# A transformer layer on one core: the first loads, the first tile, phase 3's pools and down's last terms rearranged

## The chip, the cores and the metric

The kernel runs on one core of one Trainium2 chip. The metric is the device time of one launch in microseconds (us). The core has a matrix engine (PE, with its weight loads shown as PEld), a vector engine (DVE), a scalar engine (ACT), a general engine (POOL) and a queue engine (SP) that issues most of the transfers. Each engine takes its instructions in the order in which they were written down for it.

## The reference

All data is float32. `x` is 2 x 1024 tokens of 512 features. After a layernorm, two branches read the same normed tokens and are added to `x`:

```python
xn = _layernorm(x, axis=-1)
# attention without a softmax over tokens
Q = elu(xn @ wq.T + bq) + 1; K = elu(xn @ wk.T + bk) + 1; V = xn @ wv.T + bv
KV = einsum('bhsd,bhse->bhde', K, V); K_sum = sum(K, axis=-2)
attn = (Q @ KV / (Q . K_sum + 1e-08)) @ wo.T + bo
# gated feed-forward, 1376 wide, with low-rank additions
scores = sigmoid(xn @ W_router); w = the two best of 8 experts, normed
gate = xn @ W_gate + lora_shared + sum_e w_e * lora_e     # rank 8 each
up   = xn @ W_up   + lora_shared + sum_e w_e * lora_e
hidden = silu(gate) * up
ffn = hidden @ W_down + lora_shared + sum_e w_e * lora_e
return x + attn + ffn
```

## The kernel before

Tokens go in 16 tiles of 128; `TILES` orders them so that tiles 2m and 2m+1 form a pair. The big products are not made directly: each is split in 2 x 2 blocks and made of seven block products with sums before and after (Strassen's scheme in Winograd's form), so much of DVE's, ACT's and POOL's work is block sums.

Names used below. `load_x(n)` (L146) sends tile n into a ring of four buffers. `norm(n)` (L285) writes the normed tile `xn` on DVE, after `moments`, `variances` (whose square root is on ACT, L264) and `reciprocals`. `transpose_x(n)` (L296) turns it on PE into a PSUM bank, which ACT copies into `xnT` (L302). A PSUM bank is named by a tag (`pt`, `ua`, `x`, `lo`).

**Phase 1, keys.** The loads at L150 to L159 are issued from SP in the order x0, x1, wk0, wk1, x2, wk2, wk3, x3; ACT issues the router's weights and the bias `bk`, the latter read 128 times into all partitions. Eighteen transposes of a unit matrix run on PE first (L245). Tiles 0 and 1 are projected directly (`project_k`, L344: products `pk`, bias added by DVE at L363), and POOL sums blocks of `wk` (`key_weight_sums`, L314). Pairs 1 to 7 use `k_pair` (L406) with the seven products (L424). `elu_min` and `elu_k` (L329 to L337) turn a key tile into elu(k)+1 on DVE, ACT and DVE; `accumulate` (L391) then adds its outer product with `xn` into four banks `pg`. `hooks` (L675) hang other work at named places ("n", "a", "b") of a pair: loads of the next weights, the block sums of `wq` (`query_weight_sums`), the block sums of pair 0's tokens (`pair_token_sums(0)`).

**Phase 2** forms KV, the queries, the denominators, the routing weights, and the last 96 columns of gate and up (`rest`, L1023). Its `gated_rows` stores `hr` tiles to DRAM (L1039), the last one after the second batch.

**Phase 3** (from L1454): for j in 0..4 and both batches, `unit(j, b)` (L1213) makes 2 x 128 columns of gate and up by seven outer products, five of which are split once more (`Inner`, L1168 to L1204), and stores the hidden tiles. Three pools are opened for it, in the order `up_`, `hp`, `p3`; each lies above the one before in the memory that phases 1 and 2 leave. `p3` holds `wi2` (written by POOL at L1142) and `ti56_1` (L1098); `hp` holds the hidden tiles `h`. POOL's order at the start is: `wi` sums of p=3, `wi2` sums, `ti23_0`, `token_sums_1`, `ti56_1`, `ti23_1`.

**Phase 4, down** (from L1577): four units u of 2 x 256 tokens. `emit_unit` makes seven products into seven PSUM banks (order 1, 6, 5, 2, 7, 3, 4) over five pairs of blocks of W_down (`wd`), then two of the attention's output (`kvo`); `ph` collects the hidden tiles times the experts' down factors and DVE weights it to `had` (L1616). Banks 1, 6 and 5 then go to sums (ACT L1633, POOL L1634 and L1636, DVE L1635 to L1639), while PE adds two kinds of low-rank terms to banks 2, 7, 3 and 4: `hr` (97 rows) and `had` (64 rows, rows 0 to 63 for one group of tokens and 64 to 127 for the other). DVE adds these banks to x (L1655) and SP sends the result (L1659). The next unit writes the same banks again. At the end of unit 1 the second batch's `kvo` is loaded and POOL makes its block differences (`block_diffs`, L1358) before its share of the sums.

The order on PE, DVE, ACT and POOL is that of the program text; SP's is the order in which its transfers were placed.

Of the kernel before, what the change touches and what calls it, by code (L numbers as in the profile page):

```python
# [37 lines left out]
def layer_kernel(  # L38
# [112 lines left out]
    load_x(0)  # L151
    load_x(1)
    nc.scalar.dma_start(out=wk_sb[:, :, D:], in_=by_chunk(w_router))
    bk_sb = p1.tile([P, D], F32, name="bk_sb")
    nc.scalar.dma_start(out=bk_sb, in_=bk.partition_broadcast(P))
    for c in range(NC):
        nc.sync.dma_start(out=wk_sb[:, c, 0:D], in_=wkT[ts(c, P), :])
        if c % 2:
            load_x(2 + c // 2)  # L159

# [4 lines left out]
    def load_factors():  # L165
        hold(a_in[:, 0, 0, 0:1])
        for i, a in enumerate((a_gate, a_up)):
            nc.sync.dma_start(out=a_in[:, :, i, :], in_=by_chunk(a))
        hold(ad_sb[:, 0, 0:1])
        nc.sync.dma_start(out=ad_sb[:, 0:FULL, :], in_=by_chunk(a_down[0 : FULL * P, :]))  # L170
        nc.sync.dma_start(out=ad_sb[0:REST, FULL, :], in_=a_down[RC, :])
# [110 lines left out]

    xns = {}

    def norm(n):  # L285

        k = n % 6
        xns[n] = (
            p1w.tile([P, D], F32, tag=f"xn{k}", name=f"xn{n}", bufs=1)
            if k < 4 else p2w.tile([P, D], F32, tag=f"qt{k - 2}1", name=f"xn{n}", bufs=1)  # L290
        )
        nc.vector.tensor_scalar(
            xns[n], x_sb[n], mv[:, n, 0:1], rstd[:, n : n + 1], ALU.subtract, ALU.mult
        )

    def transpose_x(n, tag="pt"):  # L296
        i = TILES[n]
        pt = bank(f"pt{i}", [P, NC, P], tag)
        for c in range(NC):
            nc.tensor.transpose(pt[:, c, :], xns[n][:, ts(c, P)], ident)  # L300
        for k in range(2):
            nc.scalar.copy(xnT[i // TPBATCH][k][:, :, ts(i % TPBATCH, P)], pt[:, 2 * k : 2 * k + 2, :])  # L302

# [35 lines left out]
    def k_tile(n):  # L339
        return p1w.tile([P, D], F32, tag="kt", name=f"kt{n}", bufs=4)  # L340

    LO, HI = slice(0, HD), slice(HD, D)

# [62 lines left out]
    def k_pair(m, late, hooks={}):  # L406
# [68 lines left out]
        nc.vector.tensor_add(ka[:, LO], ka[:, LO], lo)  # L475
        sums = pair_token_steps(2) if m == 1 else iter(())
        next(sums, None)
        ea = elu_min(ka, f"ek{na}") if m > 1 else None
        nc.vector.tensor_add(kb[:, HI], ua[:, 0:HD], bk_sb[:, HI])
        nc.vector.tensor_copy(lb, ua[:, HD:])  # L480
        ea = ea or elu_min(ka, f"ek{na}")
        list(sums)
        elu_k(ka, ea)
        eb = elu_min(kb, f"ek{nb}")
# [176 lines left out]
    for n in range(2):  # L661
# [3 lines left out]
        load_x(n + 4)  # L665
    transpose_x(0)
    wq_sums, sums1 = query_weight_sums(), token_sums(1)
# [4 lines left out]
    def routed(n):  # L672
# [3 lines left out]
        (1, "b"): [lambda: load_weights(wq_sb, wqT)],  # L676
        (2, "n"): [lambda: next(wq_sums), load_factors],
        (2, "b"): [lambda: next(wq_sums), lambda: load_weights(wv_sb, wvT)],
        (3, "n"): [lambda: next(wq_sums), lambda: next(wq_sums)],
        (3, "b"): [lambda: load_weights(wo_sb, woT), lambda: pair_token_sums(0), gather_factors, make_spread],  # L680
        (4, "b"): [lambda: fin.append(Finish(0, pg, ksum)), lambda: fin[0].copies()],
# [12 lines left out]
    for m in range(NTILE // 2):  # L694
        if m == 0:
            moments(2, 1)
            variances(2, 1)
            reciprocals()
            norm(2)
            load_x(6)  # L700
            moments(3, 1)
            ka = project_k(0, [[(0, "lo"), (1, "ua")]], lambda: transpose_x(1))
            variances(3, 1)
            key_weight_sums()
            ea = elu_min(ka, "ek0")
            reciprocals()
# [26 lines left out]

    bgu_sb = ffn.tile([2 * ER, DFF], F32, name="bgu_sb")
    for i, w in enumerate((b_gate, b_up)):
        nc.sync.dma_start(out=bgu_sb[i * ER : (i + 1) * ER, :], in_=w[0:ER, :])
# [717 lines left out]
    ph3 = ExitStack()  # L1454
    up_ = pool(ph3, "u", bufs=10)
    hp = pool(ph3, "hp", bufs=3)
    p3 = pool(ph3, "p3")
    ti56_1 = p3.tile([P, 2, 4, TH], F32, name="ti56_1")
# [118 lines left out]
    def emit_unit(u, loaded, last):  # L1577
# [44 lines left out]
        if u == 1:  # L1622
            kvo_next = load_kvo(1)
            for t in kvo_next:
                block_diffs(t)
            kvo[:] = kvo_next

# [16 lines left out]
        for pp in ((2, 7), (3, 4)):  # L1644
            for p in pp:
                g, w, _ = left[p]
                for q in range(NQ):
                    term(p, q, hr[:, g, ts(q, P)], w)
            for q in range(NQ):
                for p in pp:  # L1650
                    g, _, w = left[p]
                    rows = slice(g * ER, (g + 1) * ER)
                    term(p, q, had[rows, ts(q, P)], w[rows, :], stop=True)
        for t, d, p in ((x1, d1, 2), (x2, d2, 7), (x2, d1, 7), (x1, d2, 3), (x2, d1, 4)):
            nc.vector.tensor_add(t[:, :, d], t[:, :, d], ps[p])  # L1655
            if p == 7 and d is d1:
                continue
            first = first1 if t is x1 else first2
            nc.sync.dma_start(  # L1659
                out=out[first : first + UT, d].rearrange("(q p) d -> p q d", p=P), in_=t[:, :, d]  # L1660
            )
        if not last:
# [66 lines left out]
```

## Time and profile before

| | |
|---|---|
| median of 3 runs | 743.76 us (743.66 to 744.42) |
| the profiled execution: its own time, its span | 744.27 us, 742.5 us |
| PE busy | 730.5 us, 98% of the span |
| DVE, ACT, POOL busy | 484.6, 195.9, 161.0 us |
| from PE's last product to the span's end | 4.7 us |

The span runs from the first to the last instruction that the profiler saw; 1.77 us of the launch lie outside it. A line of a timeline gives the start, the duration, the engine, the line of the code, the operation, what it writes and reads with the sizes, how many were merged, and in brackets the idle time before it with what ended it. A line of the waits gives who waited for whom, the total, how often, and the longest. A float32 product leaves two records on PE.

### The profile page before, as it was taken

How to read it: one execution, taken by the hardware profiler on the slowest of the kernel's cores; microseconds unless marked ns; L12 is line 12 of the kernel's file. 1: busy time of each engine (PE TensorE's matmuls, PEld its weight loads, DVE VectorE, ACT ScalarE, POOL GpSimd, SP SyncE). 2: the span in 40 equal slices, each digit the busy share in tenths (PEclk: the TensorE clock that was granted, in tenths of full speed). 3: DMA queues.
4: the chain of work that ended last, by engine and by line, in shares of the span. 5: the costliest groups of instructions: out<-in, count | busy, mean ns of one | idle time of the engine just before them, and what ended most of it. 6: DMA issues, size and time to landing. Idle time of an engine off the chain costs nothing.

```text
span 742.5 us, 8737 instructions
## 1 busy us (share of the span) xinstructions
PE 730.5 (98%) x3078; PEld 489.6 (66%) x3078; DVE 484.6 (65%) x1044; ACT 195.9 (26%) x421; POOL 161.0 (22%) x206
## 2 busy tenths in 40 slices
PE   8999999999999999999999999999999999999997
PEld 6665675454433666566666666666888878888876
DVE  7799765685776688888778879879853601704303
ACT  3534413553433233333243243343000000000000
POOL 4033011202000682212113113515601003101001
PEclk9999999999999999999999999999999999999999
DMA  7333001007404001210310301353565325323001
GB/s 222 103 117 110 0 1 58 0 1 193 133 12 141 20 17 42 87 60 29 92 51 29 113 29 46 125 171 117 169 186 182 117 59 196 124 67 116 16 1 57
DMA packets 52732, 63.28 MB, mean 85 GB/s; under 512 B 9425, under 2 KB 39505, under 8 KB 52434
## 3 DMA queue, kind: packets, MB, share of 16 engines
q1 hardware_dynamic: 52018, 62.46, 26.5%
q8 instruction: 24, 0.39, 0.2%
q10 hardware_dynamic: 672, 0.28, 0.2%
q14 instruction: 18, 0.15, 0.1%
HBM read 40.97 MB, written 21.76 MB: 84 GB/s over the span
## 4 chain that ended last, share of the span: by engine, by line
PE 80%; DVE 12%; POOL 3%; issue 2%; DMA 2%; ACT 1%; SPq 0%; DVEq 0%; POOLq 0%; ACTq 0%
PE po L1586 25%; PE ab L1168 14%; PE b L1228 6%; PE pg L395 5%; PE pqu L761 4%; PE ph L1609 3%; PE kua L424 2%; PE x L1168 2%; POOL ti L1098 2%; PE pxa L840 2%; PE pqv L761 2%; PE b L1223 2%; PE pr L1062 1%; PE klo L424 1%; PE x L1223 1%
## 5 line engine op out<-in xcount | busy, mean ns | idle before, releaser
L1586 PE MATMUL po<-wd,f 128*128 128x256 f32 x560 | 122.6, 380 | 1.1 <-DVE xr L1655 1.0
L1586 PEld LDWEIGHTS po<-wd,f 128*128 128x128 f32 x560 | 105.9, 190 | 17.4 <-issue 2.1
L1228 PE MATMUL b<-t,w 128*128 128x512 f32 x160 | 83.2, 601 | 0.4 <-DVE r L1250 0.4
L395 PE MATMUL pg<-kt,xn 128*128 128x512 f32 x128 | 58.8, 594 | 0.7 <-DVE kt L337 0.5
L1616 DVE TENSOR_TENSOR had<-ph,wT 64x256 f32<-64x256 f32 x8 | 3.4, 422 | 81.3 <-PE ph L1609 81.2
L1633 ACT COPY a<-po 128x512 f32<-128x512 f32 x4 | 2.3, 587 | 186.6 <-PE po L1586 186.6
L1586 PE MATMUL po<-kvo,f 128*128 128x256 f32 x224 | 49.4, 381 | 0.0
L1250 POOL TENSOR_TENSOR r<-r,r 128x512 f32<-128x512 f32 x20 | 29.8, 1509 | 83.0 <-DVE t L1250 83.0
L1586 PEld LDWEIGHTS po<-kvo,f 128*128 128x128 f32 x224 | 42.2, 190 | 7.1 <-issue 1.2
L1168 PE MATMUL ab<-ti,wi 128*128 128x256 f32 x180 | 45.4, 379 | 0.0
L1168 PEld LDWEIGHTS ab<-ti,w 128*128 128x128 f32 x140 | 25.2, 189 | 29.8 <-DVE r L1196 9.5
L1250 DVE TENSOR_TENSOR r<-r,r 128x512 f32<-128x512 f32 x60 | 43.6, 768 | 0.0
L1168 PEld LDWEIGHTS ab<-ti,wi 128*128 128x128 f32 x180 | 34.2, 190 | 13.2 <-issue 5.0
L1168 PE MATMUL ab<-ti,w 128*128 128x256 f32 x140 | 41.2, 387 | 0.9 <-DVE r L1196 0.6
L395 PEld LDWEIGHTS pg<-kt,xn 128*128 128x128 f32 x128 | 23.1, 190 | 23.1 <-issue 20.6
L1201 ACT COPY r<-ab 128x256 f32<-128x256 f32 x50 | 18.7, 373 | 71.3 <-PE ab L1168 71.3
L1228 PEld LDWEIGHTS b<-t,w 128*128 128x128 f32 x160 | 29.2, 190 | 11.0 <-issue 5.9
L1196 DVE TENSOR_TENSOR r<-r,ab 128x256 f32<-128x256 f32 x50 | 20.9, 419 | 20.2 <-ACT r L1193 19.8
L1178 ACT COPY r<-ab 128x256 f32<-128x256 f32 x50 | 18.7, 375 | 49.5 <-PE ab L1168 44.2
L404 POOL TENSOR_TENSOR ksum<-ksum,kt 128x512 f32<-128x512 f32 x12 | 15.8, 1315 | 72.7 <-DVE lg L441 43.3
L1634 POOL TENSOR_TENSOR xr<-xr,a 128x512 f32<-128x512 f32 x4 | 5.1, 1273 | 121.1 <-ACT a L1633 81.0
L1204 DVE TENSOR_TENSOR r<-r,ab 128x256 f32<-128x256 f32 x50 | 20.9, 418 | 15.4 <-ACT r L1201 15.1
(278 smaller groups left out, 1362.2 us busy)
## 6 DMA issues: line engine op xcount, KB each, us to landing
h_dram<-h SPq DMA_DIRECT2D x40, 256.0 KB
f<-h_dram SPq DMA_DIRECT2D x20, 512.0 KB
x_ring<-in_x_dram SPq DMA_DIRECT2D x16, 256.0 KB
q_dram<-qt SPq DMA_DIRECT2D x16, 256.0 KB
f<-q_dram SPq DMA_DIRECT2D x8, 512.0 KB
xr<-in_x_dram SPq DMA_DIRECT2D x8, 512.0 KB
out_dram<-xr SPq DMA_DIRECT2D x16, 256.0 KB
w<-in_w_gate_dram SPq DMA_DIRECT2D x10, 256.0 KB
```

The source lines that it names most:

```text
L395: nc.tensor.matmul(pg[m], xns[n][:, ts(m, P)], kt, start=(j == 0), stop=(j == TPBATCH - 1))
L424: nc.tensor.matmul(out[:, 0 : w.shape[-1]], tk[p][:, k, :], w[:, k, :], start=(start and k == 0), stop=(k == 1), skip_group_check=True,)
L761: nc.tensor.matmul(banks[c], wqs[p][:, k, ts(c, P)], tsum[b][p][:, k, :], start=(start and k == 0), stop=(k == 1), skip_group_check=True,)
L1168: nc.tensor.matmul(out, w, t, start=start, stop=True, skip_group_check=True)
L1178: nc.scalar.copy(self.r[0][:, H0], self.ua)
L1196: nc.vector.tensor_add(self.r[1][:, H1], self.r[1][:, H1], self.lo)
L1204: nc.vector.tensor_add(self.r[1][:, H0], self.r[1][:, H0], self.lo)
L1223: nc.tensor.matmul(banks[m], bgu_sb[rows, cols], act[rows, :], start=starts[m], stop=True, skip_group_check=True)
L1228: nc.tensor.matmul(pb[m], ws[m][:, A_OF[p], ts(k, P)], tsum[b][p][:, k, :], start=start, stop=True, skip_group_check=True)
L1250: eng.tensor_add(to[m], t[m], v[m])
L1586: nc.tensor.matmul(ps[p][:, q, :], lhsT, rhs, start=start, stop=stop, skip_group_check=True)
L1609: nc.tensor.matmul(ph[g * ER : (g + 1) * ER, :], a, f[:, g, :], start=(n == 0), stop=(n == len(chunks) - 1), skip_group_check=True,)
```

## The change

- The first transfers alternate: x0, wk0, wk1, x1, wk2, wk3, x2, x3. The bias `bk` is loaded as one row, ahead of the router's weights on ACT; a product of a row of ones with it spreads it over the partitions in a bank, from which ACT copies it back into `bk_sb`.
- Tile 0 is normed in two halves, and its four transposes go into two banks, so that each copy waits for its own two.
- Tile 0's transposes stand right after its norm. In pair 0, tile 2's reciprocals and norm come after `project_k(0)` and not before moments 3. `elu_min` and `elu_k` of pair 1 come earlier. The sums of `wq` and `pair_token_sums(0)` move to later pairs; `bgu_sb` gets a memset ahead of its loads, which holds them back; the hold of `a_in` covers both halves.
- `p3` is opened before `hp`.
- In down, all `had` terms come first and then all `hr` terms, in the order 7, 2, 3, 4; DVE's sums follow in the order 7, 7, 2, 3, 4. The last unit's last sum and store go in two halves. `kvo`'s second load stays where it was, and its block differences come after the sums.

```diff
     load_x(0)
-    load_x(1)
+    bk_sb = p1.tile([P, D], F32, name="bk_sb")
+    nc.scalar.dma_start(out=bk_sb[0:1, :], in_=bk.unsqueeze(0))
     nc.scalar.dma_start(out=wk_sb[:, :, D:], in_=by_chunk(w_router))
-    bk_sb = p1.tile([P, D], F32, name="bk_sb")
-    nc.scalar.dma_start(out=bk_sb, in_=bk.partition_broadcast(P))
     for c in range(NC):
         nc.sync.dma_start(out=wk_sb[:, c, 0:D], in_=wkT[ts(c, P), :])
-        if c % 2:
-            load_x(2 + c // 2)
+        if c == 1:
+            load_x(1)
+    load_x(2)
+    load_x(3)
...
-        hold(a_in[:, 0, 0, 0:1])
+        hold(a_in[:, 0, :, 0:1])
...
-        nc.vector.tensor_scalar(
-            xns[n], x_sb[n], mv[:, n, 0:1], rstd[:, n : n + 1], ALU.subtract, ALU.mult
-        )
+        for half in (LO, HI) if n == 0 else (slice(0, D),):
+            nc.vector.tensor_scalar(
+                xns[n][:, half], x_sb[n][:, half], mv[:, n, 0:1], rstd[:, n : n + 1], ALU.subtract, ALU.mult
+            )
...
-        pt = bank(f"pt{i}", [P, NC, P], tag)
+        pt = [bank(f"pt{i}", [P, NC, P], tag)] * 2
+        if n == 0:
+            pt[1] = bank("pt0_1", [P, NC, P], "ua")
         for c in range(NC):
-            nc.tensor.transpose(pt[:, c, :], xns[n][:, ts(c, P)], ident)
+            nc.tensor.transpose(pt[c // 2][:, c, :], xns[n][:, ts(c, P)], ident)
         for k in range(2):
-            nc.scalar.copy(xnT[i // TPBATCH][k][:, :, ts(i % TPBATCH, P)], pt[:, 2 * k : 2 * k + 2, :])
+            nc.scalar.copy(xnT[i // TPBATCH][k][:, :, ts(i % TPBATCH, P)], pt[k][:, 2 * k : 2 * k + 2, :])
...
         sums = pair_token_steps(2) if m == 1 else iter(())
+        ea = elu_min(ka, f"ek{na}")
         next(sums, None)
-        ea = elu_min(ka, f"ek{na}") if m > 1 else None
         nc.vector.tensor_add(kb[:, HI], ua[:, 0:HD], bk_sb[:, HI])
         nc.vector.tensor_copy(lb, ua[:, HD:])
-        ea = ea or elu_min(ka, f"ek{na}")
+        elu_k(ka, ea)
         list(sums)
-        elu_k(ka, ea)
...
-    transpose_x(0)
+        if n == 0:
+            transpose_x(0)
+
+            pbk = bank("pbk", tag="x")
+            nc.tensor.matmul(pbk, ones[0:1, :], bk_sb[0:1, :], start=True, stop=True)
+            nc.scalar.copy(bk_sb, pbk)
...
-        (2, "n"): [lambda: next(wq_sums), load_factors],
-        (2, "b"): [lambda: next(wq_sums), lambda: load_weights(wv_sb, wvT)],
-        (3, "n"): [lambda: next(wq_sums), lambda: next(wq_sums)],
-        (3, "b"): [lambda: load_weights(wo_sb, woT), lambda: pair_token_sums(0), gather_factors, make_spread],
+        (2, "n"): [load_factors],
+        (2, "b"): [lambda: load_weights(wv_sb, wvT)],
+        (3, "n"): [lambda: next(wq_sums)],
+        (3, "b"): [lambda: load_weights(wo_sb, woT), gather_factors, make_spread],
+        (4, "n"): [lambda: next(wq_sums), lambda: next(wq_sums)],
+        (6, "n"): [lambda: next(wq_sums)],
+        (7, "n"): [lambda: pair_token_sums(0)],
...
             variances(2, 1)
-            reciprocals()
-            norm(2)
-            load_x(6)
             moments(3, 1)
             ka = project_k(0, [[(0, "lo"), (1, "ua")]], lambda: transpose_x(1))
             variances(3, 1)
             key_weight_sums()
+            reciprocals()
+            norm(2)
+            load_x(6)
             ea = elu_min(ka, "ek0")
...
     bgu_sb = ffn.tile([2 * ER, DFF], F32, name="bgu_sb")
+    hold(bgu_sb[:, 0:1])
...
     up_ = pool(ph3, "u", bufs=10)
+    p3 = pool(ph3, "p3")
     hp = pool(ph3, "hp", bufs=3)
-    p3 = pool(ph3, "p3")
...
         if u == 1:
-            kvo_next = load_kvo(1)
-            for t in kvo_next:
-                block_diffs(t)
-            kvo[:] = kvo_next
+            kvo[:] = load_kvo(1)
...
         for pp in ((2, 7), (3, 4)):
-            for p in pp:
-                g, w, _ = left[p]
-                for q in range(NQ):
-                    term(p, q, hr[:, g, ts(q, P)], w)
             for q in range(NQ):
                 for p in pp:
                     g, _, w = left[p]
                     rows = slice(g * ER, (g + 1) * ER)
-                    term(p, q, had[rows, ts(q, P)], w[rows, :], stop=True)
-        for t, d, p in ((x1, d1, 2), (x2, d2, 7), (x2, d1, 7), (x1, d2, 3), (x2, d1, 4)):
-            nc.vector.tensor_add(t[:, :, d], t[:, :, d], ps[p])
+                    term(p, q, had[rows, ts(q, P)], w[rows, :])
+        for p in (7, 2, 3, 4):
+            g, w, _ = left[p]
+            for q in range(NQ):
+                term(p, q, hr[:, g, ts(q, P)], w, stop=True)
+        for t, d, p in ((x2, d2, 7), (x2, d1, 7), (x1, d1, 2), (x1, d2, 3), (x2, d1, 4)):
+            first = (first1 if t is x1 else first2)
+            for q in (slice(0, 1), slice(1, 2)) if last and p == 4 else (slice(0, NQ),):
+                nc.vector.tensor_add(t[:, q, d], t[:, q, d], ps[p][:, q, :])
+                if p != 7 or d is d2:
+                    nc.sync.dma_start(
+                        out=out[first : first + UT, d].rearrange("(q p) d -> p q d", p=P)[:, q, :], in_=t[:, q, d]
+                    )
+        if u == 1:
+            for t in kvo:
+                block_diffs(t)
```

## The prediction, made before the changed kernel had run

> **What bounds the kernel now.** I read the page's busy times first, then who waited for whom on PE, then the timelines around each part that the diff touches.
>
> ```profile
> span 742.5 us, 8737 instructions
> ...
> PE 730.5 (98%) x3078; PEld 489.6 (66%) x3078; DVE 484.6 (65%) x1044; ACT 195.9 (26%) x421; POOL 161.0 (22%) x206
> ```
>
> PE is the bound: it idles 12 us of 742.5. No other engine's work counts unless PE waits for it. The waits of PE say where:
>
> ```profile
> PE pt L300 <- DVE xn L292: 1.2, 1, 1.2
> PE po L1586 <- DVE xr L1655: 1.0, 2, 0.8
> ...
> PE pg L395 <- DVE kt L337: 0.5, 1, 0.5
> ```
>
> The page lists only stalls of PE; an unhidden weight load stays inside "busy". So I compare starts as well: a product of 256 columns leaves two records 0.2165 us apart, of 512 columns 0.43 apart. What a stretch takes beyond that is lost.
>
> The start (timeline, DVE, ACT and PE mixed):
>
> ```profile
> 6.69 1.09 PE L300 MATMUL pt<-ident,xn 128*128 128x128 f32 x4 [1.21 <-DVE xn L292]
> ...
> 8.24 3.90 PE L356 MATMUL pk<-wk_sb,xnT 128*128 128x256 f32 x12 [0.46 <-ACT xnT L302]
> ...
> 8.77 0.55 DVE L292 TENSOR_SCALAR xn<-x_ring,mv,rstd 128x512 f32<-128x512 f32 x1
> ...
> 11.60 1.47 DVE L292 TENSOR_SCALAR xn<-x_ring,mv,rstd 128x512 f32<-128x512 f32 x1
> ...
> 13.81 0.74 DVE L363 TENSOR_TENSOR kt<-pk,bk_sb 128x256 f32<-128x256 f32 x2
> ```
>
> The first four pk records start about 0.43 apart, the later ones 0.2165: PE runs at half speed until about 10.1. The second norm takes 0.55 with POOL idle, the third 1.47 beside POOL's sums of L319.
>
> Phase 3 begins with a late POOL (POOL's timeline, then PE's):
>
> ```profile
> 250.17 0.46 POOL L1142 TENSOR_TENSOR wi<-w 128x128 f32<-128x128 f32 x1 [3.56 <-DMA r_dram<-hr]
> ```
> ```profile
> 272.13 0.70 PE L1168 MATMUL ab<-ti,w 128*128 128x256 f32 x2 [0.39 <-DVE r L1196]
> ...
> 274.55 1.12 PE L1228 MATMUL b<-t,w 128*128 128x512 f32 x2 [0.42 <-DVE r L1250]
> ...
> 276.11 0.70 PE L1168 MATMUL ab<-t,w 128*128 128x256 f32 x2 [0.43 <-DVE r L1204]
> ```
>
> The end of down's second unit, where POOL's block differences stand in front of the x sums:
>
> ```profile
> 621.36 1.02 POOL L1359 TENSOR_TENSOR kvo<-kvo 128x256 f32<-128x256 f32 x1 [45.59 <-DMA kvo<-kvo_dram]
> ...
> 632.40 3.11 DVE L1655 TENSOR_TENSOR xr<-xr,po 128x512 f32<-128x512 f32 x5 [9.48 <-POOL xr L1634]
> ...
> 633.14 1.13 PE L1586 MATMUL po<-wd,f 128*128 128x256 f32 x4 [0.78 <-DVE xr L1655]
> ```
>
> The last unit's low-rank terms and end:
>
> ```profile
> 733.68 0.73 PEld L1586 LDWEIGHTS po<-bd_sb,had 64*128 64x128 f32 x8 [0.33 <-issue]
> ...
> 734.75 0.73 PEld L1586 LDWEIGHTS po<-wdr,hr 97*128 97x128 f32 x4 [0.33 <-issue]
> ...
> 737.84 1.29 DVE L1655 TENSOR_TENSOR xr<-xr,po 128x512 f32<-128x512 f32 x2 [1.03 <-PE po L1586]
> ```
>
> **What the Trainium skill says.** "TensorE: Matmul & The Clock Gate", Part 1: the array's clock is halved until it has been busy for some 3.4 us; the trace agrees (0.43 against 0.2165, up to 10.1). Its Part 3 says that products on different row groups run side by side; the trace has the had pairs starting 0.01 apart. "SBUF — State Buffer", Who interferes with whom: VectorE and GpSimd share a port pair as an exclusive lock; the 1.47 agrees.
>
> **The change, part by part** (losses plus, gains minus, us).
>
> *Start.* Split norm: a half should take half of 0.55, so the first transpose starts 0.25 earlier, at 6.42, the fourth at 7.07 (0.2167 apart, as the 18 warm-up transposes). Before, xnT's copy alone decided when pk starts, at 8.24; with its own bank the first copy would start at 7.08 and free pk at 7.5. But the bias product now stands ahead of pk on PE: two records of 512 columns, 0.43 each warm, 0.86 each at half speed, from 7.28 to 9.0. By 10.1 pk has 2.6 records done instead of 4: 0.3 late. Bound if the clock were fast: pk at 8.15, 0.1 early.
> ACT copies the bias behind that (0.59, from the copies of L1633: 9.2 to 9.8), and tile 1's square root is queued behind the copy: 9.83 instead of 7.58. DVE follows: tile 1's norm moves from 8.77 to 11.0, and wk, ahead of x2 and x3 and without the 256 KB bias broadcast, lets POOL's sums start near 7.5 instead of 10.17 (an estimate: the 1.6 MB up to wk's end, at the 0.19 MB per half microsecond that the DMA view has from 6 to 9 us), so this norm meets them: 1.47, to 12.5. Then moments 2 and 3 (0.9 and 0.2 between) to 14.5, the two kt adds to 15.2, the variance 0.15, and now reciprocals and norm 2 (0.95+0.55), formerly done while DVE would have waited for pk, ek (0.42), reciprocals and norm 3 (1.5), kt adds (0.75), L337 (0.68): pg starts near 20.3 instead of 18.44, +1.9. The router's small packets no longer leave before x0's: -0.15. I take **+1.7**, bounds -0.3 (nothing of it on the path, split norm kept) and +2.8. Later x tiles, reordered among the sb loads on SP's queue, have over 5 us to spare.
>
> *Key pairs.* In pair 3 PE restarts at 57.20 where 55.10+4x0.43 gives 56.82, because two wq sums (0.68, 0.88) precede L455; the klo at 63.35 should start at 63.0, behind pair_token_sums(0) on DVE (4x0.42). One sum stays in pair 3, the rest moves. In pair 1 pg starts 0.3 late at 36.13 behind L337, which now comes 1.2 earlier: **-1.0**. Covers of what moves: at pair 4, L455 would end by 70.9 and PE wants its bank at 71.76; at pair 6 0.68 goes into a DVE wait; at pair 7 the token sums fill 1.7 of a 2.77 wait. If pair 4's cover fails, 0.4 returns: bounds -1.2 and -0.3. bgu's 0.69 MB goes from 11 us to 127 us behind a memset of 0.06; its first reader runs after 170, and SP has w_0 behind it, wanted at 240: 0.
>
> *Pools.* wi2 lay where hr's last store still read; p3 now lies 6 KB lower, and in the built program's order of waits it asks for stores issued some 10 us earlier. POOL gains 3.56 and its last ti ends near 269 instead of 272.5. PE's three gaps, by starts: 272.13 for 271.7, 274.55 for 273.96, 276.11 for 275.4, so 1.7 with the loads; this unit and the next take 55.6 where later pairs of units take 54.47, so about 1.1 can be had. **-1.0**, bounds -1.3 and -0.2 (DVE late on its own). The last hr store now meets h's first tile: it landed at 250, h is written at 266.
>
> *Unit 1.* Differences behind the x sums: L1655 no longer waits 9.48. Twelve wd records from 629.50 end at 632.10, restart came at 633.14; four more give 634.01, restart 634.46: **-1.5**. The differences are wanted only at unit 2's end, 30 us on. Bounds -1.5, -1.0.
>
> *Low-rank order.* Before, hr, had, hr, had: four pairs of 0.2165 are 0.87, but had-to-hr takes 1.07 and the last had to wd (628.44 to 629.50) 1.06; hr-to-had costs 0.1. Excess 0.2+0.2+0.19=0.6 a unit; with one had block 0.2 to 0.3. 0.35 to 0.4 a unit, four units: **-1.4**, bounds -1.6 and -0.6. Bank 2's sum is now third on DVE, yet ends 0.4 before PE stops, 3 before PE wants it.
>
> *End.* PE's end to the span's end is 742.5-737.80=4.7. Then: two sums (1.29), SP issue, transfer, completion. Now bank 3's sum runs under PE's last four records; after PE stands the second half's 0.42 (one started earlier), and 128 KB rather than 256 is sent last (0.4 less at 340 GB/s), but one more issue of 0.37 queues on SP. 1.29+0.04-0.9 = 0.4, and 0.4: **-0.8**, bounds -1.2 and 0.
>
> **Sum**: 1.7-1.0-1.0-1.5-1.4-0.8 = -4.0. The profiled execution took 744.27 (1.77 outside the span), 0.51 above the median of 743.76; I take the difference to the median: 743.76-4.0 = **739.8**.
>
> **Rivals.** Within 0.2% (1.5 us) a measurement can't tell from no change: 742.3 to 745.2.
> - *The start is free* (0.20): the bias product and its copy fit under other waits, or PE's clock is up early. For: PE had a 0.46 gap there. Against: ACT's order. Start -0.2: 743.76-5.9 = 737.9.
> - *The stalls only change names* (0.12): the pools' gain is kept by DVE (-0.2) and the clock comes up later, costing 2.8 at the start; 743.76-2.1 = 741.7, about half of this case above 742.3.
> - *Slower* (0.06): in the merged had block the pairs no longer run side by side. 8 pairs x 4 units x 0.2165 = 6.9 more, 743.76-4.0+6.9 = 746.7; it decides from 0.17 lost on each pair. Against: q by q the groups still alternate.
>
> **How the numbers follow.** The sum as it stands has 0.62, between 738.4 and 741.2. Faster: 0.62+0.20+0.05 = 0.87; same 0.07; slower 0.06. From 737.6 to 742.0 the range leaves out the slower case, some half of the renamed stalls and the far end of the free start.
>
> **What would show it.** Right: PE's pg near 20; POOL's wi without a wait at 246; no PE wait for L1655 at unit 1; one had block of eight pairs in about 2.0; 3.9 from PE's end to the span's end. Wrong: pg before 18.5; ti's last sum past 271; had records 0.2165 apart singly; a wait of PE in pairs 4 to 7.

## The result, and the profile after

The changed kernel takes 739.35 us (median of 6 runs, 739.22 to 740.92); the kernel before, run beside it, 743.72 (6 runs, 743.07 to 744.42). The ratio is 0.9943, with a 95% interval of 0.9931 to 0.9956: 4.2 us less. The profiled execution took 739.22 us, its span is 737.5.

The page of the kernel after:

```profile
span 737.5 us, 8743 instructions
...
PE 728.4 (99%) x3080; PEld 490.7 (67%) x3080; DVE 485.8 (66%) x1047; ACT 195.9 (27%) x422; POOL 160.2 (22%) x206
```

PE has two records more (the bias product) and 2.1 us less busy time; its idle time (span less busy) fell from 12.0 to 9.1 us. So 2.1 of the 5.0 us between the two spans lay inside "busy", in time that the list of waits doesn't have. The waits of PE after:

```profile
PE pt L305 <- DVE xn L295: 1.3, 1, 1.3
PE b L1239 <- DVE t L1261: 0.7, 1, 0.7
...
PE klo L427 <- DVE kt L478: 0.2, 1, 0.2
```

The two waits for L1655 (now L1666) are gone. The wait of `b` for `t` and that of `klo` are new at these places. The start, all engines mixed:

```profile
6.32 0.67 PE L305 MATMUL pt<-ident,xn 128*128 128x128 f32 x4 [1.27 <-DVE xn L295]
6.92 1.16 PE L672 MATMUL pbk<-bk_sb,ones 1*128 1x512 f32 x2
...
8.00 4.51 PE L359 MATMUL pk<-wk_sb,xnT 128*128 128x256 f32 x12
...
8.59 0.21 ACT L265 ACTIVATE sd<-ve 128x1 f32<-128x1 f32 x1
...
19.00 2.41 PE L398 MATMUL pg<-kt,xn 128*128 128x512 f32 x5 [0.54 <-DVE kt L342]
```

The bias product runs at full speed (two records in 1.16), and `pk` behind it at half speed for the most part: twelve records in 4.51, where 2.90 is their full speed in later traces. ACT's square root for tile 1, behind the copy of the bias from its bank, is at 8.59 (7.58 before), DVE's norm of tile 1 at 9.77 (8.77). `pg` starts at 19.00, 0.56 later than before.

Phase 3, first DVE's two sums of 512 columns in the kernel before, then POOL, DVE and PE in the kernel after:

```profile
258.35 1.85 DVE L1250 TENSOR_TENSOR r<-r,r 128x512 f32<-128x512 f32 x2
```
```profile
246.50 0.76 POOL L1153 TENSOR_TENSOR wi<-w 128x128 f32<-128x128 f32 x1
...
258.28 3.35 DVE L1261 TENSOR_TENSOR r<-r,r 128x512 f32<-128x512 f32 x2
...
262.62 1.12 PE L1239 MATMUL b<-t,w 128*128 128x512 f32 x2 [0.74 <-DVE t L1261]
```

POOL's `wi` sums no longer wait. But POOL is now at its sums of 512 columns (`ti`) when DVE makes its own two, and these take 3.35 instead of the 1.85 of before, when POOL was at sums of 256 columns.

Unit 1's end and the last unit:

```profile
617.53 1.27 POOL L1642 TENSOR_TENSOR xr<-xr,a 128x512 f32<-128x512 f32 x1 [42.35 <-ACT a L1641]
...
627.37 9.88 PE L1597 MATMUL po<-wd,f 128*128 128x256 f32 x45
...
730.95 3.34 DVE L1666 TENSOR_TENSOR xr<-xr,po 128x512 f32<-128x512 f32 x6 [3.82 <-PE po L1597]
...
732.47 1.03 PE L1597 MATMUL po<-wdr_diff,hr 97*128 97x256 f32 x4
```

POOL makes the x sums at once, and the 45 `wd` records run without a gap. The last record ends at 733.50, 4.0 ahead of the span's end.

Where the 5.0 us between the two spans lie, read from the starts of the same PE instructions in both traces (after minus before):

| up to | difference there | step |
|---|---|---|
| first `pg` | +0.56 | start +0.56 |
| last product of pair 3 | -0.90 | |
| first `pg` of pair 5 | -0.10 | key pairs -0.66 |
| first product of phase 3 | -0.07 | |
| first `ph` of unit 0 | -1.44 | pools -1.37 |
| first `ph` of unit 1 | -1.84 | low-rank order, unit 0: -0.40 |
| `ph` of unit 3 | -4.11 | units 1 and 2: -0.40, -0.41; unit 1's stall: -1.46 |
| PE's end | -4.30 | last unit -0.19 |
| span's end | -5.0 | end -0.7 |

### The profile page after: what moved, and what is told of

The parts are those of the page before. It is cut to its first block, busy times and chain, and to the rows that moved or that the text cites. A ratio compares the mean times of both kernels' runs of the same rounds, so it can differ in the third digit from the quotient of the medians.

```text
span 737.5 us, 8743 instructions
## 1 busy us (share of the span) xinstructions
PE 728.4 (99%) x3080; PEld 490.7 (67%) x3080; DVE 485.8 (66%) x1047; ACT 195.9 (27%) x422; POOL 160.2 (22%) x206
## 4 chain that ended last, share of the span: by engine, by line
PE 85%; DVE 12%; ACT 1%; issue 1%; DMA 0%; DVEq 0%
PE po L1597 26%; PE ab L1179 16%; PE b L1239 8%; PE pg L398 5%; PE pqu L772 4%; PE ph L1620 3%; PE x L1179 3%; PE b L1234 2%; PE pxa L851 2%; PE pqv L772 2%; PE pr L1073 2%; PE kua L427 2%; PE x L1234 1%; DVE r L1261 1%; DVE xn L295 1%
## 5 line engine op out<-in xcount | busy, mean ns | idle before, releaser
L1212 ACT COPY r<-ab 128x256 f32<-128x256 f32 x50 | 18.6, 372 | 70.9 <-PE ab L1179 70.9
L1239 PEld LDWEIGHTS b<-t,w 128*128 128x128 f32 x160 | 29.2, 190 | 11.3 <-issue 5.9
L1189 ACT COPY r<-ab 128x256 f32<-128x256 f32 x50 | 18.6, 373 | 48.4 <-PE ab L1179 47.1
```

The lines of the kernel that those rows point to most:

```text
L1189: nc.scalar.copy(self.r[0][:, H0], self.ua)
L1212: nc.scalar.copy(self.r[0][:, H1], self.ua)
L1239: nc.tensor.matmul(pb[m], ws[m][:, A_OF[p], ts(k, P)], tsum[b][p][:, k, :], start=start, stop=True, skip_group_check=True)
```

## Each part alone

Six kernels make one part of the change each in the kernel before. Their edits are hunks of the diff above; they are named by their first or decisive lines. A median of several runs here is uncertain by some 0.7 us, so the timelines decide, and the medians are a check on the whole. (The ratios are those on record and need not be the quotient of the two medians beside them.)

**The start.**

```diff
+    nc.scalar.dma_start(out=bk_sb[0:1, :], in_=bk.unsqueeze(0))
...
+        for half in (LO, HI) if n == 0 else (slice(0, D),):
...
+            nc.tensor.matmul(pbk, ones[0:1, :], bk_sb[0:1, :], start=True, stop=True)
...
             key_weight_sums()
+            reciprocals()
+            norm(2)
```

> The kernel before with the start's part alone: the alternating loads, the bias by one product, tile 0 normed in halves, tile 2's norm behind project_k. Theory A (PE's clock): the first pg product starts 0.4 to 0.7 us later than before's 18.44, as in the kernel after, because PE runs at half speed under more of pk's records (two records 0.43 apart up to about 11.5 us); the median is 744.3 us. Theory B (the order on ACT and DVE): the same start, but pk's records at full speed from 10 us on and DVE's norm of tile 2 as what pg waits for; the median is the same 744.3, so that the two part in the trace: under A the granted clock or the spacing of pk's records shows half speed, under B DVE has no wait for PE between 10 and 19 us. If the start is no part of the loss, pg starts at 18.44 or earlier and the median is 743.6 or less.

Measured: 744.24 against 743.76, ratio 1.0003 (0.9992 to 1.0013). `pg` starts at 18.47, but with `pk` at full speed:

```profile
8.14 2.90 PE L359 MATMUL pk<-wk_sb,xnT 128*128 128x256 f32 x12
11.55 0.66 PE L305 MATMUL pt<-ident,xn 128*128 128x128 f32 x4 [0.52 <-DVE xn L295]
```

The edit is the same as in the kernel after, and PE's speed under `pk` is not. Theory A as I had put it, a cost that the edit brings each time, is wrong; with PE fast, DVE's order is what `pg` waits for, as theory B has it: from the norm of tile 1 at 9.91 to the `kt` that `pg` waits for, DVE has no idle time. But `pg` is not 0.4 to 0.7 later, as both theories had it; it is where it was before. The start varies with the execution, which the kernels that share the old start show as well (under "What the start depends on").

**The key pairs.**

```diff
+        (4, "n"): [lambda: next(wq_sums), lambda: next(wq_sums)],
+        (6, "n"): [lambda: next(wq_sums)],
+        (7, "n"): [lambda: pair_token_sums(0)],
```

> The kernel before with the key pairs' part alone: the order of elu in pair 1, the moved sums of wq, the moved token sums of pair 0 and the memset ahead of bgu_sb. Theory A: the gain of pairs 1 to 3 (1.4 us, klo of pair 3 at 62.0 instead of 63.35) is given back by 0.8 in pair 4, where the two wq sums stand ahead of tiles 10 and 11's moments on DVE, which ACT's square root and, behind it on ACT, the copies of xnT wait for; phase 3 starts at 244.2, and the median is 743.1. Rival: the 0.8 was lost to the start's changed loads; then pair 4 gives nothing back here, phase 3 starts at 243.4 and the median is 742.3.

Measured: 743.79 against 743.76, ratio 0.9993 (0.9986 to 1.0001). The start cost 1.19 in this execution (`pg` at 19.63), so I read differences to the kernel before, less 1.19: up to pair 3's last product -1.48, by pair 5 back to -0.65. Theory A holds, the rival doesn't. The absolute start of phase 3 (0.54 later than before) missed because of the start. What happens in pair 4, first before, then in the kernel after:

```profile
72.53 0.20 ACT L264 ACTIVATE sd<-ve 128x2 f32<-128x2 f32 x1 [0.33 <-DVE ve L262]
...
74.81 0.43 DVE L384 TENSOR_TENSOR t<-xnT,xnT 128x256 f32<-128x256 f32 x1 [1.08 <-ACT xnT L302]
```
```profile
72.83 0.20 ACT L265 ACTIVATE sd<-ve 128x2 f32<-128x2 f32 x1 [1.54 <-DVE ve L263]
73.06 1.28 ACT L268 ACT_TABLE_LOAD   x1
...
75.12 0.42 DVE L387 TENSOR_TENSOR t<-xnT,xnT 128x256 f32<-128x256 f32 x1 [1.54 <-ACT xnT L307]
```

The two sums (1.28 in all, from 69.37) delay the variance; ACT's square root waits 1.54 for it instead of 0.33, and a table load and the copies of `xnT` (74.46) stand behind the root. DVE's token sums wait for those copies, and `klo` at 77.18 for DVE. The 1.08 us in which DVE stood idle ahead of L384 before looked like room, and grew to 1.54 by DVE's own sums.

**The pools.**

```diff
+    p3 = pool(ph3, "p3")
     hp = pool(ph3, "hp", bufs=3)
-    p3 = pool(ph3, "p3")
```

> The kernel before with p3 opened ahead of hp and nothing else. Theory A: POOL's wi sums start at 246.5 without a wait and three gaps of PE between 272 and 277 go (1.7 us), but POOL's token sums now run beside DVE's first two sums of 512 columns at 258.3, which take 3.3 us instead of 1.85, and PE waits some 0.7 for DVE at 262.6: net 0.85 gained, median 742.9. Rival: the wait at 262.6 belongs to another part of the change and is not there, net 1.7 gained, median 742.0.

Measured: 742.39 against 743.76, ratio 0.9975 (0.9966 to 0.9984). In its trace the difference to the kernel before goes from +1.75 ahead of phase 3 to +2.77 at the new wait and to +0.63 at 281 us, +0.38 at the first `ph`: 1.1 and then 1.4 gained. The wait is there:

```profile
264.45 1.12 PE L1228 MATMUL b<-t,w 128*128 128x512 f32 x2 [0.76 <-DVE t L1250]
```

Theory A holds in kind, with more gained than I had put. The last 0.25, most of it near 442 us, comes with the order of the pools too; why is open. Together they make 1.37, by which the median fell too.

**Unit 1's block differences.**

```diff
-            for t in kvo_next:
-                block_diffs(t)
...
+        if u == 1:
+            for t in kvo:
+                block_diffs(t)
```

> The kernel before with the block differences of kvo behind the x sums at the end of unit 1, and nothing else. Theory: the two gaps of PE at 633.14 and 634.46 (1.04 and 0.36 by the starts) go and nothing takes their place, since POOL has the differences done long before the end of unit 2: 1.4 gained, median 742.3. Rival: the x sums on POOL then wait for ACT and DVE anyway and only one of the gaps goes: 0.4 to 0.8 gained, median 743.1.

Measured: 743.02 against 744.10, ratio 0.9987 (0.9979 to 0.9995). The difference to the kernel before falls by 1.47 between the ends of unit 0 and of unit 1: the theory holds. The stall that it removes is not always that large. From the first `ph` of unit 1 to that of unit 2 it is 53.38 here; in the traces with the old order of POOL and of the low-rank terms it is longer by 1.48 (before), 1.45 (25 transposes, below), 1.30 (end alone), 1.04 (keys alone), 0.65 (start alone) and 0.64 (pools alone), 1.09 on the average, where the medians have 1.08. PE's listed waits for L1655 or its like sum to 1.0 us in the profiled execution of before, 0.8 in that with the end alone, 0.5 with the key pairs alone, 0.2 with the pools or the start alone. In the first two, POOL's last differences wait another 1.06 and 0.97 us for the second transfer of `kvo`, in these others 0.26 or not at all: the landing goes with the size, so it sets it at least in part.

**The low-rank order.**

```diff
+                    term(p, q, had[rows, ts(q, P)], w[rows, :])
+        for p in (7, 2, 3, 4):
...
+                term(p, q, hr[:, g, ts(q, P)], w, stop=True)
+        for t, d, p in ((x2, d2, 7), (x2, d1, 7), (x1, d1, 2), (x1, d2, 3), (x2, d1, 4)):
```

> The kernel before with the low-rank terms of down in two groups (had first, then hr in the order 7, 2, 3, 4) and DVE's sums in the order 7, 7, 2, 3, 4. Theory: from the first low-rank product to the first product after them PE takes 5.49 us instead of 5.87 in units 0 to 2, 0.38 a unit for fewer changes between 97 and 64 rows, and about as much in the last: 1.4 gained, were it not for unit 1: there bank 2's sum is now third on DVE, behind a sum that waits for POOL, which is late, so PE's wait of 0.78 grows by 0.4 to 1.0. Median 742.7 to 743.2. Rival: the 0.38 is no matter of the order but of the waits of unit 1 and is not found in units 0 and 2; median 743.8.

Measured: 744.23 against 744.10, ratio 1.0004 (0.9996 to 1.0012). By the starts: unit 0 -0.40, unit 2 -0.40, last unit -0.19, and unit 1 +0.69, in which -0.40 is hidden under a stall that grew by about 1.1, a little more than expected:

```profile
632.78 2.48 DVE L1655 TENSOR_TENSOR xr<-xr,po 128x512 f32<-128x512 f32 x4 [5.41 <-POOL xr L1636]
...
634.12 6.09 PE L1586 MATMUL po<-wd,f 128*128 128x256 f32 x27 [2.29 <-DVE xr L1655]
```

Bank 2's sum is third on DVE and stands behind one that waits for POOL's second x sum. So this part needs the one before it: alone the two give +0.1 and -1.1 us on the medians, and in the kernel after the same order costs nothing at unit 1. The rival falls. The median missed the forecast by 1 us, and the stall explains only 0.1 of it; the span of this trace is 0.7 under that of before, as its stretches have it, so the rest of the miss lies in the other executions and stays open. What the order saves is seen in the starts of records: ahead of and behind each block of `had` two records start 0.31 and 0.31 or 0.32 apart instead of 0.2165, some 0.2 lost at each change into or out of the 64-row block. Before, a unit has four such changes, now two; between the 128-row `kvo` and the 97-row `hr` there is no such loss (0.22). One thing I hadn't expected: from PE's end (736.73 + 1.03) to the span's end (741.8) it is 4.0 us here, with no halving.

**The end.**

```diff
+            for q in (slice(0, 1), slice(1, 2)) if last and p == 4 else (slice(0, NQ),):
```

> The kernel before with the last unit's last sum and store in halves and nothing else. Theory: from PE's last product to the end of the span 4.0 to 4.3 us instead of 4.7; bank 3's terms still end together with bank 4's, so one sum more than in the changed kernel stands after PE's end: 0.5 gained, median 743.2. Rival: the end is set by the last issue and its completion, which the halving doesn't shorten: 0.0, median 743.7.

Measured: 743.92 against 744.10, ratio 0.9997 (0.9988 to 1.0005). From PE's last product (738.71 + 0.38) to the span's end (743.63) it is 4.55 us against 4.66. So the halving is worth 0.1, less than I had expected; the order of the banks, which ends bank 3 before bank 4, is worth 0.64 (4.02 in the trace of the low-rank order alone).

## What the start depends on

Six profiled executions share the old start (before, keys, pools, unit 1, low-rank and end alone): their first `pg` is at 18.44, 19.63, 20.20, 18.82, 18.74 and 19.96 (an expectation below counts seven; they are six). Four share the new one: 19.00, 18.47, 20.93 and 20.57. In the pools' trace, with the old code:

```profile
8.33 5.57 PE L356 MATMUL pk<-wk_sb,xnT 128*128 128x256 f32 x12 [0.67 <-ACT xnT L302]
```

All twelve `pk` records are at half speed here (no two start less than 0.43 apart, the first at 8.33, the last at 13.25); the profile of before, from which I had taken the clock's schedule, has the earliest `pg` of the six. The Trainium skill ("TensorE: Matmul & The Clock Gate", Part 1) says that PE's activity is watched in a free-running window, so that the same program has more or fewer slow products from run to run; these traces agree: with the same old start from four (before) to all twelve (pools) of `pk` are slow, with the same new one from none (start alone) to nine. I had drawn on that part for the halved clock and passed over this sentence. The trace of before had shown it too: its 18 transposes of the unit matrix keep PE at work without a gap from 1.37 to 5.48, and all of them, like tile 0's four, start 0.21 apart; in the traces where the clock has come up, products of this size start 0.11 apart. There it did not come up in 4.1 us of work, while in the kernel after it did, after some 3.1 us, and fell again.

From the first `pg` on, the traces hardly differ but by what was edited. To phase 3's first product it is 226.35 to 226.38 in the seven traces with the old key pairs and 225.72 to 225.75 in the four with the new ones; from there to the first `ph` it is 308.08 to 308.34 in the seven with the old pools and 306.96 to 306.99 in the six that have nothing but the new ones there; a unit of down takes 52.98 instead of 53.38. What differs from one execution to the next is the start, and with the old order at unit 1 the stall there.

Two kernels fill PE's idle time ahead of tile 0:

```diff
-    WARM = 18
+    WARM = 25
```

> The changed kernel with 25 instead of 18 transposes of the unit matrix ahead of tile 0, so that PE has no idle time of 1.27 us before tile 0's transposes. Theory A (PE's clock falls after that idle time): pk's twelve records take 2.7 us instead of 4.51, the second tile's transposes start at about 11 instead of 12.34, pg at 18.2 instead of 19.0, the median falls by 0.7 to 738.6. Theory B (DVE's and ACT's order sets pg): pk is faster but pg still starts at 19.0 and the median stays at 739.3. If the seven transposes run at half speed to their end they end at 7.0 and tile 0 is 0.6 late: 739.9.

> The kernel before with 25 instead of 18 transposes of the unit matrix ahead of tile 0. Seven traces of the kernel before and of kernels that share its start have the first pg product between 18.4 and 20.2 us, by how long PE runs at half speed under pk. Theory A (the clock falls in the idle time ahead of tile 0's transposes): with that time filled pk's twelve records take 2.9 us or less, pg starts at 18.2 to 18.6, and the median is 0.8 lower, at 743.0; against the changed kernel with the same 25 (pg at 18.33) the rest of the start part is then worth 0.0 to 0.2. Theory B (what helped the changed kernel is its own order of loads and norms): pg stays between 18.8 and 20.2 and the median at 743.8.

Measured: 738.56 us (737.86 to 739.28) for the changed kernel, ratio to before 0.9919 (0.9906 to 0.9932); 743.47 against 744.13 for the kernel before, 0.9989 (0.9981 to 0.9997). With the old start:

```profile
8.19 2.90 PE L356 MATMUL pk<-wk_sb,xnT 128*128 128x256 f32 x12 [0.78 <-ACT xnT L302]
...
17.61 2.84 PE L395 MATMUL pg<-kt,xn 128*128 128x512 f32 x6 [0.54 <-DVE kt L337]
```

`pk` takes 2.90 in both and `pg` starts at 17.61 with the old start, 18.33 with the new one. Theory A holds for both kernels, theory B of the second doesn't. Filled, the old start is even 0.7 ahead in this pair (my expectation, 18.2 to 18.6 for the old one, was too late); in the changed kernel the 25 ended at 7.0, as the last case of the expectation has it, but cost less than put there. With 22 (below) the new start has 17.54 and 18.39, so I don't call the difference between the starts shown. The five executions of the changed kernel with 25 still lie 1.4 us apart: filling took the slow products of `pk` away, not the whole spread.

That idle time brings the clock down is best seen in two traces in which it came up at the same moment, the kernel after and that with 22 transposes: in both the transposes' starts turn from 0.21 to 0.11 apart at 4.5. PE then stood idle for 1.27 in the one and 0.93 in the other until tile 0 came (6.32 and 6.42). In the first the clock fell at 7.9 and `pk` was slow, in the second it did not fall. The length alone doesn't decide: in the trace of the end alone PE was idle there for 0.88, the clock had not yet come up, and all of `pk` was slow. The view of the second:

```profile
6.42 0.67 PE L305 MATMUL pt<-ident,xn 128*128 128x128 f32 x4 [0.93 <-DVE xn L295]
...
8.07 2.90 PE L359 MATMUL pk<-wk_sb,xnT 128*128 128x256 f32 x12
```

## The price of pairs that don't run side by side

```diff
-        for pp in ((2, 7), (3, 4)):
-            for q in range(NQ):
-                for p in pp:
+        for pp in ((2, 3), (7, 4)):
+            for p in pp:
+                for q in range(NQ):
```

> The changed kernel with the had terms in the order of banks 2, 3, 7, 4, so that neighbours on PE use the same 64 rows but for one place. If the pairs run side by side only because neighbours use different rows, each unit's sixteen records take sixteen times 0.2165 instead of eight times: 1.5 to 1.7 more a unit, 6.0 to 6.9 in all, median 745.4 to 746.2. That is the price of the slower case of the prediction. If PE reaches over more than its neighbour, nothing changes: 739.35.

Measured: 743.94 us, ratio to before 0.9998 (0.9988 to 1.0008), 4.6 more than the changed kernel, of which its start has a part (`pg` at 20.57, 1.57 later). The `had` blocks of unit 0, first of the changed kernel, then of this one:

```profile
568.90 1.34 PE L1597 MATMUL po<-bd_sb,had 64*128 64x256 f32 x9
...
570.83 2.86 PE L1597 MATMUL po<-wdr,hr 97*128 97x256 f32 x12
```

```profile
570.46 2.10 PE L1597 MATMUL po<-bd_sb,had 64*128 64x256 f32 x12
...
573.35 2.86 PE L1597 MATMUL po<-wdr,hr 97*128 97x256 f32 x12
```

From the first `had` to the first `hr` it is 1.93 and 2.89: 0.97 a unit (the same in units 1, 2 and 3), 3.9 in all and not the 6.9 of the prediction's slower case. Twelve records take 1.94, which is 0.16 each and not 0.2165: around the one change of rows, from bank 3 to bank 7, records still overlap (two start at 571.42 and 571.43). The rival that PE reaches over more than its neighbour is half right.

## Towards a version that beats both

**Pair 4 mended.**

```diff
-        (4, "n"): [lambda: next(wq_sums), lambda: next(wq_sums)],
-        (4, "b"): [lambda: fin.append(Finish(0, pg, ksum)), lambda: fin[0].copies()],
+        (4, "b"): [lambda: next(wq_sums), lambda: next(wq_sums), lambda: fin.append(Finish(0, pg, ksum)), lambda: fin[0].copies()],
```

> The changed kernel with the two sums of wq of pair 4 moved from place n to place b, behind the variance of tiles 10 and 11 on DVE, where DVE waits for ACT's copy of xnT. Theory A (ACT's square root, 1.28 us of table load and the copies of xnT stand behind the variance): pair 4 takes 0.8 less, its last klo waits no longer, the difference between the first pg of pair 3 and phase 3's first product (244.75 - 50.29 = 194.46) falls to 193.7, and the median from 739.35 to 738.6. Theory B (DVE simply has too much work in pair 4): the sums delay the token sums behind them just as much, and the difference stays within 0.2.

Measured: 739.99 (738.40 to 740.29), ratio to before 0.9939 (0.9927 to 0.9951). From pair 3's first `pg` (52.22) to phase 3's first product (245.82) it is 193.60: theory A. The median doesn't show it, since this kernel's start was late (`pg` at 20.93 in the profile). In its trace:

```profile
75.17 0.63 ACT L307 COPY xnT<-pt 128x256 f32<-128x256 f32 x2
...
75.86 0.42 DVE L387 TENSOR_TENSOR t<-xnT,xnT 128x256 f32<-128x256 f32 x1
```

The same two sums (74.66 to 75.9) now lie where DVE would wait for ACT, and the wait is gone.

**With 22 transposes as well.** The edit is the one above and `WARM = 22`.

> The changed kernel with 22 transposes of the unit matrix instead of 18 and the two sums of wq of pair 4 at place b. Theory A: the 22 end at 6.3, when the first half of tile 0 is there, so PE has no gap and loses nothing to them; pk's twelve records take 2.9, pg starts at 18.0 to 18.3, pair 4 gives back nothing (phase 3's first product less pair 3's first pg: 193.6 instead of 194.46); median 739.35 - 0.8 - 0.85 = 737.7. Rival: with the chain on PE shorter by 0.6 DVE sets pg, which stays at 18.3 to 18.5, and the clock needs longer than the 22 last, so that pk is at half speed in part: median 738.3 to 738.6.

Measured: 737.20 us (736.89 to 737.44), ratio to before 0.9910 (0.9896 to 0.9923). `pg` starts at 17.54, 1.46 ahead of the changed kernel's, and phase 3's first product at 242.44, 2.3 ahead. It has the lowest median of all; its upper bound of 0.9923 lies below the changed kernel's 0.9931.

**POOL held as well.**

```diff
+    def late_sums(u2):
+        nc.gpsimd.tensor_copy(after_u2, u2[:, 0:1])
+        list(token_sums_56(nc.gpsimd, 1, ti56_1))
+        list(token_sums_23(1, slot(7, [2, 4, TH], "ti23_1")))
...
         add(V, u2, u2, u1)
+        if j == 0 and b == 0:
+            late_sums(u2[1])
```

> As the kernel with 22 transposes and the later sums of wq, and POOL's last eight token sums of phase 3's start put behind DVE's two sums of 512 columns (a copy of one column on POOL reads the second one's result). Theory A: DVE's two sums take 1.3 us instead of 3.35 since POOL stands still, PE's wait of 0.74 for t goes, POOL's last sum ends near 270 instead of 268.3, still in time: 0.7 to 0.9 less than that kernel, median 736.9. Rival: POOL is then late for the second batch's products, and the gaps at 272 to 276 come back: 0.5 to 1.0 more than that kernel, or no difference if both happen.

Measured: 737.27 us (736.96 to 738.24), ratio to before 0.9913 (0.9899 to 0.9927), no difference to the kernel without it on the medians.

```profile
256.81 1.28 DVE L1260 TENSOR_TENSOR r<-r,r 128x512 f32<-128x512 f32 x2
...
267.16 3.10 DVE L1260 TENSOR_TENSOR t<-t,r 128x512 f32<-128x512 f32 x2
...
270.98 0.70 PE L1178 MATMUL ab<-ti,w 128*128 128x256 f32 x2 [0.78 <-DVE r L1206]
```

With POOL still, DVE's two sums take 1.28 instead of 3.35, and PE's wait at 262.6 is gone: the meeting of the two engines is its cause. But POOL's last sums, now from 266.3 to 269.7, meet DVE's next pair of the kind, which takes 3.10 (1.28 in the changed kernel), and behind it PE waits 0.78. Of the rival the outcome holds, both happened; its reason doesn't, since what is late at 270.98 is DVE and not POOL. From phase 3's first product to the first `ph` it is 307.24, and 306.96 without the hold: the meeting was moved, at a cost of 0.28, and not removed.

## Why the prediction was right, and where it wasn't

The time was 0.45 us under the forecast of 739.8. In the pair of profiled executions the sum was -5.0 instead of -4.0, and the first step alone accounts for this 1.0, with 1.7 put where 0.56 was measured. That the median came closer than the pair is luck in part: the pair is one draw of a start that moves `pg` from 18.47 to 20.93 with the new order (four traces), and a stall at unit 1 that was larger in the kernel before's profile than in any other. Of the six runs of the changed kernel the slowest, 740.92, lies above the forecast. One of the signs of being wrong that the prediction named did come, a wait of PE in pairs 4 to 7 (0.19 for `klo` in pair 4), and one of its signs of being right did not (`pg` near 20; it was 19.00). By its steps:

- **Start, +1.7.** Measured +0.56, in one pair; the part alone changes the time by no more than the measurement tells. The step failed where it took the clock of one execution for a schedule: "0.86 each at half speed, from 7.28 to 9.0" for the bias product, which took 1.16 in all and ended near 8. (A half of the norm took 0.41 and not half of 0.55, which tile 0, there 0.24 earlier, made up for.) All that hangs on it came early: the square root at 8.59 for 9.83, the norm of tile 1 at 9.77 for 11.0. Half speed then came over `pk`, where the step had it end at 10.1. The order on ACT that it named is there (the bank's copy ahead of the square root, DVE behind it). This was closer to the first rival, a start that is free.
- **Key pairs, -1.0.** Measured -0.66. The gain up to pair 3 was -1.46; pair 4 gave 0.80 back. The step did ask what pair 4's sums cost, and bounded it with 0.4, by looking at the next sum on DVE (L455, which was in fact on time within 0.2). It didn't follow the variance over to ACT and back.
- **Pools, -1.0.** Measured -1.37. POOL's gain and its last sum's end (268.3 for 269) came as stated, the three gaps too; the step did not see that an earlier POOL meets DVE elsewhere (1.01 lost at 262.6), nor 0.25 gained later, whose cause is open. The section of the Trainium skill that the prediction used for the norm ("SBUF — State Buffer", Who interferes with whom) would have told it: a DVE instruction with two SBUF inputs meets POOL's reads, one with at most one SBUF input doesn't, unless it runs in a two-port mode. The traces agree: a sum of 512 columns from two SBUF tiles took 0.64 with POOL still and 1.67 beside its sums (POOL's own 1.72 for 1.27), and the sum of an SBUF tile and a bank that followed 0.64 beside POOL at work. The norm has one SBUF tile and met POOL all the same (0.55 with POOL still, 1.47 beside its sum); by that section it must run in such a mode, which no run here shows by itself.
- **Unit 1, -1.5.** Measured -1.46, alone -1.47. The size belongs to these executions; in five others with the old order the same stall cost 0.64 to 1.45, so it was largest in the very execution that the step was read from.
- **Low-rank order, -1.4.** Measured -1.40 (0.40, 0.40, 0.41, 0.19). The step's "excess" reading of record starts holds: the changes into and out of the 64-row blocks cost, and are fewer. It put "hr-to-had" at 0.1, which is 0.2 like the others: the excess was 0.8 and not 0.6 a unit, of which half is left.
- **End, -0.8.** Measured -0.7. The step gave half of it to the sums that stand behind PE's end and half to a shorter last transfer; 0.64 comes with the order of the banks, 0.1 with the halves of sum and store.

The slower rival's mechanism is real, and it didn't occur, since the two groups alternate; forced, its price was 3.9 and not 6.9.

## What to carry to other kernels

The profile of one execution is one draw: before an edit is costed against a clock, a landing or a stall in it, ask which of its times would come out the same next time, and remove what varies (here, for the most part, by keeping PE at work) before tuning around it. An engine's idle time is room only if the work that ends it doesn't hang on what is put in; follow the moved instruction's result over the other engines and back. An engine that is freed early does its work beside other work: look at what it will meet.

## What I had not expected of the hardware

- PE's half-speed spell at the start differs from one execution to the next though the program's start is the same: `pk`'s twelve records took from 3.90 to 5.57 us in the six traces with the old start and from 2.90 to 4.89 in the four with the new one. `pk` was at full speed in all four traces with more transposes, and in one of these ten.
- Where the clock had come up in the warm-up and fell again, the spell at half speed ended by itself 3.4 us later, with PE at work: 7.9 to 11.3 in the kernel after (8.3 to 11.7 in that of unit 1, 8.6 to 12.0 in that of the low-rank order). The view of after has it: at half speed from 0.12 ahead of 8.00 until 0.29 behind 11.00 (columns: the stretch, PE busy, PE's busy time, clock, DMA share, GB/s).

```profile
7.00:8.00 1.00, 1.00 (x2) 0.94 1.11 377
8.00:9.00 1.00, 1.00 (x3) 0.50 1.14 265
...
11.00:12.00 1.00, 1.00 (x5) 0.85 0.11 22
```

  In the view of before the column stays at 1.00, though the records there are 0.43 apart as well. This is no reading: that trace has no record of the clock ahead of 10.31, where its records turn from half to full speed, and the column shows 1.00 where there is none. For the first microseconds the spacing of records is the surer sign.
